# Macaron blocks on one core: router weights first, centered attention weights after the first routing, both norms of the late feed-forward ahead of its wide products

## The chip, the cores and the metric

One NeuronCore of a Trainium2 chip runs the whole program in one launch. The metric is the device time of one execution in microseconds (us), lower is better. A profiled execution also leaves a trace of every engine: TensorE (PE, with its weight loads as PEld), VectorE (DVE), ScalarE (ACT), GpSimd (POOL) and SyncE (SP), which issues most DMAs.

## The reference

The input is 4 x 1024 tokens with 128 channels, float32. Four layers follow one another; each is a half feed-forward, an attention, and the same half feed-forward again, all on a residual x. Each part first normalizes over the channels, without weights:

```python
def _layernorm(x, axis=-1, eps=1e-05):
    m = jnp.mean(x, axis=axis, keepdims=True)
    v = jnp.var(x, axis=axis, keepdims=True)
    return (x - m) / jnp.sqrt(v + eps)
...
    x = x + 0.5 * _L0_ffn_ref(_layernorm(x, axis=-1), ...)
    x = x + _L0_attn_ref(_layernorm(x, axis=-1), ...)
    x = x + 0.5 * _L0_ffn_ref(_layernorm(x, axis=-1), ...)
    x = x + 0.5 * _L1_ffn_ref(_layernorm(x, axis=-1), ...)
    x = x + _L1_attn_ref(_layernorm(x, axis=-1), ...)
    x = x + 0.5 * _L1_ffn_ref(_layernorm(x, axis=-1), ...)
```

Layer 0's feed-forward is a mixture of 8 experts of width 512: each token's normalized channels are multiplied by the router's weights, the two highest experts are taken, and their outputs are added with softmax weights. Layer 0's attention runs within a token, over its 16 heads of 8 channels. Layer 1's feed-forward is gated, `silu(gate) * up` of width 384 and a product down, with integer weights scaled by 1/127. Layer 1's attention is a softmax attention of 16 heads over 1024 tokens with rotated queries and keys. Layers 2 and 3 (another mixture, linear attentions, a recurrence) are not touched by the change.

## The kernel before

The residual lies in SBUF, channels on the partitions, as four tiles X[b] of 128 x 1024, one for each batch b. A norm is made on PE: a product with the centering matrix `c0["center"]` takes the mean away, ScalarE squares the result, products with a column of 1/128 give the variance, ScalarE takes the square root and VectorE the reciprocal; products with a broadcast of it (against the identity) spread it over the channels, and VectorE multiplies.

**Start of the program** (`run`). SP's queue gets the DMAs in the order in which they are written: the constants c0 (463.5 KB), the four x (512 KB each), then what the first two stages need: l0s (the router's weights, 128 x 8, 4 KB), l0a (layer 0's attention, 256 KB), l1f (layer 1's feed-forward, 576 KB) and more. l1f is read into a pool of its own, l1int, which is closed again when VectorE has scaled its three matrices (L601). Then the pool of the experts is opened. `moe["both"]` (L1387 to L1389) holds the centering matrix and, beside it, the centered router's weights, so that one product of X with it gives centered channels and logits at once.

**Layer 0** (`layer0`, `macaron`). A routing (`route`) takes one or two batches: products with "both", squares on ScalarE (L303), the square root (L305), scaled rows written to DRAM (L309), and then small VectorE steps that find each token's two experts and a list of blocks of 128 slots. An experts' task takes one block after another: SP loads the expert's weights (e_w, 578 KB), POOL gathers the rows (L454), PE and ScalarE compute, POOL scatters the result (L480). A combine reads both results of each token back and adds them to X. There are three groups of batches in each of the two mixtures: (0), (1), (2, 3) before the attention and (0, 1), (2), (3) after it. `centered` multiplies layer 0's attention weights with the centering matrix (`m["wqkvc"]`, read by `l0_attn` as the tasks "middle0" to "middle3").

The order in which these tasks' instructions are written comes from `lanes`: every task is a generator that yields its cost, each lane has a clock, and the lane with the lowest clock goes next. A task starts when the tasks it names are done, at a clock no lower than the lowest of the other active lanes. A scheduler then orders the instructions of every engine by what it expects to be ready, with the written order as priority, and places tiles when their buffers come free.

**Layer 1's attention** (`l1_attn`). PE's order is written by hand here (`manual_schedule`); the other engines' is not. Before the loop, `prepare(0)` makes batch 0's norm and projections, a generator with eleven yields; `spread` then lays queries and keys out with DMAs. The loop runs over units k: `greatest` finds the scores' row maxima (PE, and two VectorE reductions at L740 for each k), and eleven units later (LEAD) `scores` and `values` compute the exponentials and sums. "two" is a PSUM tile of two banks with two buffers; "s" has one bank and three buffers; "e" is an SBUF tile of 128 x 512 with ten buffers.

Layer 1's first feed-forward of the last batch (`self.late`) is not done in layer 0 but fed into this stage: `feed(b, hf)` is a generator for one half of the batch's columns. Its calls do, in order: centering, square and a copy (1); variance and reciprocal (2); broadcast and the normalized xn (3); a gate, a Silu, an up product and a multiplication for each of three hidden slices (4 to 6, the wide products); nothing (7); the product down and the addition to X (8). While `prepare(0)` runs, one call of a feed follows each of its yields from the third on; in the loop, one call of the feed at the head of the list follows each k, and one that is finished is removed.

Of the kernel before, what the change touches and what calls it, by code (L numbers as in the profile page):

```python
# [18 lines left out]
B, S, D = 4, 1024, 128  # L19
# [190 lines left out]
class Macaron:  # L210
# [446 lines left out]
    def l1_attn(self, m, c1, f):  # L657
# [6 lines left out]
        with ExitStack() as ctx:  # L664
# [150 lines left out]
            def feed(b, hf):  # L815
                c = slice(hf * HALF, (hf + 1) * HALF)
                bank, one = lambda: self.t(p2, [P, HALF], "s"), lambda: self.t(wp, [P, HALF], "e", bufs=10)
                cen, sq, xc = bank(), one(), one()
                self.mm(cen, self.c0["center"], self.X[b][:, c])
                nc.scalar.activation(sq, cen, AF.Square)  # L820
                v.tensor_copy(xc, cen)
                yield
                var = bank()[:, 0:4]
                for i in range(4):
                    self.mm(var[:, i : i + 1], sq[:, i * P : (i + 1) * P], self.c0["mean"][:, 0:1])
                std, r = self.t(self.lnp, [P, 4], "fstd"), self.t(self.lnp, [P, 4], "frstd")
                nc.scalar.activation(std, var, AF.Sqrt, bias=self.eps_ln)
                v.reciprocal(r, std)
                yield
                bc, xn, hs = bank(), one(), []  # L830
                for i in range(4):
                    self.mm(bc[:, i * P : (i + 1) * P], r[:, i : i + 1].to_broadcast([P, P]), self.c0["ident"])
                v.tensor_tensor(xn, xc, bc, ALU.mult)
                yield
                for i in range(HIDC):
                    g, u, s = bank(), bank(), one()
                    self.mm(g, f["wg"][:, i, :], xn)
                    nc.scalar.activation(s, g, AF.Silu)
                    self.mm(u, f["wu"][:, i, :], xn)
                    hs.append(one())  # L840
                    v.tensor_tensor(hs[i], s, u, ALU.mult)
                    yield
                yield
                o = bank()
                for i in range(HIDC):
                    self.mm(o, f["wd"][:, i, :], hs[i], start=i == 0, stop=i == HIDC - 1)
                self.add_half(b, c, o)

            late = [feed(b, hf) for b in self.late for hf in range(2)]
            for n, _ in enumerate(prepare(0)):  # L850
                if late and n >= 2:
                    next(late[0], None)
            for z in va:
                nc.gpsimd.memset(z, 0.0)
                nc.gpsimd.memset(z[:, :, :, 0:1], 1.0)
# [437 lines left out]
        self.lanes(blocks, back, *more(route))  # L1293

    def layer0(self, moe, m, right, enter, ffn):
        m["wqkvc"] = self.centered(m["wqkv"], 3 * D)
        early = right.enter_context(ExitStack())
        pa, pf = enter(early, "l0a"), enter(right, "l1f0", side="left")
        side, main = self.side, self.main
        self.late = [B - 1]  # L1300

        def swap():

            early.close()
            self.l1_rings(enter(self.rings, "l1rings", 1))
            yield 0

        def more(route):
            attn = lambda b, *after: (f"middle{b}", after, lambda: self.l0_attn(side, pa, m, b))
            last = lambda b, ps: (f"last{b}", (f"combine1{b}",), ffn(pf, ps, b))  # L1310
            return (
                [
                    route(0, (0,), ps=main), route(0, (1,)), route(0, (2, 3)),
                    *[attn(b, f"combine0{b}") for b in range(B)],
                    ("swap", (), swap), *[last(b, side) for b in range(B) if b not in self.late],
                ],
                [route(1, (0, 1), "middle0", "middle1", "combine03"), route(1, (2,), "middle2"), route(1, (3,), "middle3")],
            )


        groups = [(0,), (1,), (2, 3)], [(0, 1), (2,), (3,)]
        marks = {(0, (0,)): "_1", (0, (1,)): "_2", (0, (2, 3)): "_0", (1, (0, 1)): "_0", (1, (2,)): "_1", (1, (3,)): "_2"}
        self.macaron("l0", moe, AF.Gelu, groups, marks, more)
# [30 lines left out]
    def run(self, stages):  # L1354
        nc = self.nc
        self.X, self.ring, self.rings, self.late = [], {}, ExitStack(), []
        self.c0 = self.load("c0")
        for b in range(B):
            X = self.t(self.res, [P, S], f"x{b}")
            nc.sync.dma_start(out=X, in_=self.x[:, b * S : (b + 1) * S])  # L1360
            self.X.append(X)
        self.eps_ln = self.t(self.res, [P, 1], "eps_ln")
        nc.gpsimd.memset(self.eps_ln, LN_EPS)
        self.eps_gn = self.t(self.res, [P, 1], "eps_gn")
        nc.gpsimd.memset(self.eps_gn, GN_EPS)

        needs = {
            "l0": ("l0s", "l0a", "l1f"), "l1_attn": ("l1a", "c1"), "l2": ("l2s", "l2a", "c2"),
            "l3": ("l3f", "l3a", "c3"),
        }  # L1370
        tags = {"l1a": "attn_w", "l3a": "attn_w", "c1": "attn_c", "c2": "attn_c", "c3": "attn_c"}
        have = {}

        def weights(name):
            if name not in have:
                have[name] = self.l1_weights() if name == "l1f" else self.load(name, tag=tags.get(name))
            return have[name]

        sb = lambda name, bufs=2, **k: self.tc.tile_pool(name=name, bufs=bufs, reuse_waits="tile", **k)
        for n, name in enumerate(stages):  # L1380
            for s in stages[n : n + 2]:
                for w in needs[s]:
                    weights(w)
            if name in ("l0", "l2"):
                with self.psum("main", 4) as self.main, self.psum("side", 4) as self.side, sb(name + "moe") as self.fp:
                    moe = dict(weights(name + "s"))
                    moe["both"] = self.t(self.res, [P, P + NE], "both", bufs=2)  # L1387
                    nc.vector.tensor_copy(moe["both"][:, 0:P], self.c0["center"])
                    nc.scalar.copy(moe["both"][:, P:], self.centered(moe["rw"], NE))  # L1389
                    with ExitStack() as right:  # L1390
                        enter = lambda stack, name, bufs=2, side="right": stack.enter_context(sb(name, bufs, side=side))
                        m = dict(weights(name + "a"))
                        ffn = lambda wp, ps, b: lambda: self.l1_ffn(ps, wp, weights("l1f"), b)
                        if name == "l2":
                            self.c2 = weights("c2")
                        if name == "l0":
                            self.layer0(moe, m, right, enter, ffn)
                        else:
                            self.layer2(moe, m, right, enter, ffn)
            elif name == "l1_attn":  # L1400
                with sb("ln1") as self.lnp:
                    if not self.ring:
                        self.l1_rings(self.rings.enter_context(sb("l1rings", 1, side="right")))
                    self.l1_attn(weights("l1a"), weights("c1"), weights("l1f") if self.late else None)
                    self.rings.close()
            else:
                f, t, c3 = self.l3_ffn_weights(weights("l3f")), self.l3_time_weights(weights("l3a")), weights("c3")
                self.layer3(f, t, c3)
        self.rings.close()
        for b in range(B):  # L1410
            nc.sync.dma_start(out=self.out[:, b * S : (b + 1) * S], in_=self.X[b])
# [36 lines left out]
```

## Time and profile before

| | before |
|---|---|
| median of 3 runs | 3091.13 us (3089.98 to 3100.73) |
| the profiled execution, whole time | 3093.76 us |
| its span in the trace | 3092.0 us |
| mean granted TensorE clock | 0.915 |
| PE busy | 2709.1 us (88%) |
| VectorE, ScalarE, POOL busy | 59%, 53%, 25% |
| layer 0: from the first gather on POOL to the last scatter | 36.16 to 839.24 us |
| layer 1's attention: first scores to last exponential | 881.6 to 1935 us |

The page's slices, forty of equal length (77.3 us each), give the busy tenths of each engine, and the granted clock of TensorE in tenths of full speed:

```profile
PE   6868538778889999999999999998989996999997
PEld 5756416665643333333333333567878884334333
DVE  3586986864356776776677774362665632455763
ACT  4655425657715665565565666454444553344442
POOL 4666307553400000000000000047434562000110
PEclk8988768889989999999999999999989997798997
```

In each line a 9 stands for 90% or more. A line of the trace's timeline, as shown further on, gives the start in us, the length in us, the engine, the line of the code (L231 is the matmul helper `mm`), the operation, what it writes and reads with the tiles' names, its shapes and a count, and in brackets how long the engine had been idle before it and whose end released it.

### The profile page before, as it was taken

How to read it: one execution, taken by the hardware profiler on the slowest of the kernel's cores; microseconds unless marked ns; L12 is line 12 of the kernel's file. 1: busy time of each engine (PE TensorE's matmuls, PEld its weight loads, DVE VectorE, ACT ScalarE, POOL GpSimd, SP SyncE). 2: the span in 40 equal slices, each digit the busy share in tenths (PEclk: the TensorE clock that was granted, in tenths of full speed). 3: DMA queues.
4: the chain of work that ended last, by engine and by line, in shares of the span. 5: the costliest groups of instructions: out<-in, count | busy, mean ns of one | idle time of the engine just before them, and what ended most of it. 6: DMA issues, size and time to landing. Idle time of an engine off the chain costs nothing. (4 is left out here: it accounts for less than half of the span.)

```text
span 3092.0 us, 47511 instructions
## 1 busy us (share of the span) xinstructions
PE 2709.1 (88%) x17694; PEld 1564.1 (51%) x17694; DVE 1834.9 (59%) x3215; ACT 1623.9 (53%) x3633; POOL 780.5 (25%) x732
## 2 busy tenths in 40 slices
PE   6868538778889999999999999998989996999997
PEld 5756416665643333333333333567878884334333
DVE  3586986864356776776677774362665632455763
ACT  4655425657715665565565666454444553344442
POOL 4666307553400000000000000047434562000110
PEclk8988768889989999999999999999989997798997
DMA  7766316563500000000000000058665783000000
GB/s 247 220 182 189 113 52 199 165 201 108 156 14 5 5 7 4 5 6 5 19 5 6 1 1 1 20 179 267 203 191 170 229 283 103 1 1 0 7 7 14
DMA packets 122886, 277.57 MB, mean 90 GB/s; under 512 B 18016, under 2 KB 67296, under 8 KB 122528
## 3 DMA queue, kind: packets, MB, share of 16 engines
q1 hardware_dynamic: 101792, 231.77, 24.2%
q0 software_dynamic: 20864, 42.77, 4.9%
q8 instruction: 140, 2.29, 0.3%
q14 instruction: 90, 0.74, 0.1%
HBM read 238.43 MB, written 31.85 MB: 87 GB/s over the span
## 5 line engine op out<-in xcount | busy, mean ns | idle before, releaser
L740 DVE TENSOR_REDUCE nm<-two 128x2 f32<-128x1024 f32 x512 | 626.0, 1224 | 280.8 <-PE s L231 270.2
L763 ACT ACTIVATE e<-s 128x512 f32<-128x512 f32 x1024 | 555.8, 595 | 404.0 <-PE s L231 400.8
L468 ACT ACTIVATE e_h<-bank,e_w 128x128 f32<-128x128 f32 x1304 | 448.7, 367 | 397.2 <-PE bank L231 382.6
L231 PE MATMUL s<-qm,kz 32*128 32x512 f32 x2048 | 633.8, 642 | 0.8 <-ACT e L763 0.8
L231 PE MATMUL bank<-e_x,e_w 128*128 128x128 f32 x2608 | 535.5, 309 | 87.1 <-ACT e_h L468 54.7
L231 PE MATMUL two<-kz,qz 32*128 32x512 f32 x2048 | 578.0, 647 | 21.0 <-DVE nm L740 4.6
L454 POOL DMA_INDIRECT e_xg<-rows,g_source x326 | 330.6, 1014 | 753.7 <-DVE g_target L421 342.7
L231 PEld LDWEIGHTS bank<-e_x,e_w 128*128 128x128 f32 x2608 | 410.6, 203 | 166.9 <-ACT e_h L468 100.6
L231 PE MATMUL bank<-e_w,e_h 128*128 128x128 f32 x2608 | 463.3, 293 | 27.1 <-ACT e_h L468 17.2
L480 POOL DMA_INDIRECT res<-e_y,g_target x326 | 365.3, 1121 | 258.4 <-DVE e_y L479 106.4
L231 PEld LDWEIGHTS bank<-e_w,e_h 128*128 128x128 f32 x2608 | 379.3, 202 | 50.6 <-ACT e_h L468 30.7
L231 PE MATMUL o<-e,va 128*32 128x256 f32 x4096 | 328.3, 392 | 0.1
L231 PEld LDWEIGHTS o<-e,va 128*32 128x32 f32 x4096 | 81.0, 108 | 389.6 <-issue 369.6
L231 PEld LDWEIGHTS two<-kz,qz 32*128 32x128 f32 x2048 | 153.8, 184 | 228.9 <-issue 162.7
L231 PEld LDWEIGHTS s<-qm,kz 32*128 32x128 f32 x2048 | 206.9, 183 | 11.3 <-issue 7.7
L460 DVE COPY e_x<-bank 128x128 f32<-128x128 f32 x326 | 92.8, 285 | 192.0 <-PE bank L458 176.1
L479 DVE TENSOR_TENSOR e_y<-bank,e_w 128x128 f32<-128x128 f32 x326 | 93.9, 288 | 183.2 <-PE bank L231 163.3
L728 POOL COPY va<-vd 128x256 f32<-128x256 f32 x16 | 6.7, 431 | 624.6 <-PE o L231 537.9
L1177 POOL TENSOR_TENSOR z<-st,r 128x512 f32<-128x512 f32 x32 | 46.2, 1443 | 417.8 <-DVE st L1170 334.3
L458 PE MATMUL bank<-c,e_xg 128*128 128x128 f32 x326 | 96.5, 298 | 42.5 <-DMA e_xg<-rows,g_source 38.9
L468 ACT ACT_TABLE_LOAD x53 | 68.0, 1283 | 22.8 <-PE bank L231 16.6
L546 DVE TENSOR_TENSOR prod<-qkv 128x2048 f32<-128x2048 f32 x32 | 73.1, 2284 | 4.7 <-ACT qkv L538 4.7
(325 smaller groups left out, 3467.1 us busy)
## 6 DMA issues: line engine op xcount, KB each, us to landing
e_w<-in_l0m_dram SPq DMA_DIRECT2D x170, 578.0 KB
e_w<-in_l2m_dram SPq DMA_DIRECT2D x156, 578.0 KB
c_y<-res SPq DMA_DIRECT2D x32, 512.0 KB
rows<-g_xt SPq DMA_DIRECT2D x16, 512.0 KB
e_xg<-rows,g_source POOLq DMA_INDIRECT x326
res<-e_y,g_target POOLq DMA_INDIRECT x326
x<-in_x_dram SPq DMA_DIRECT2D x4, 512.0 KB
qz<-qd SPq DMA_DIRECT2D x64, 32.0 KB
```

What stands on the lines that cost most here:

```text
L231: self.nc.tensor.matmul(out, lhsT, rhs, start=start, stop=stop)
L454: nc.gpsimd.indirect_dma_start(out=xg, out_offset=None, in_=rows[:, :], in_offset=at(source[:, k : k + 1]))
L458: nc.tensor.transpose(tp, xg, self.c0["ident"])
L460: nc.vector.tensor_copy(x, tp)
L468: nc.scalar.activation(h[:, fc, :], o[:, fc, :], func, bias=w[:, 2 * FC * P + fc : 2 * FC * P + fc + 1])
L479: nc.vector.tensor_tensor(y, o, w[:, MOE_W - D :], ALU.add)
L480: ins = nc.gpsimd.indirect_dma_start(out=res[:, :], out_offset=at(target[:, k : k + 1]), in_=y, in_offset=None)
L546: v.tensor_tensor(pr, q.unsqueeze(2).to_broadcast(sh), k.unsqueeze(1).to_broadcast(sh), ALU.mult)
L728: nc.gpsimd.tensor_copy(va[n % RING][:, :, :, 1 : 1 + HD], dense[b, "vd"][:, :, 32 * g4 : 32 * g4 + 32].rearrange("p t (h d) -> p t h d", ...
L740: v.tensor_reduce(nm[:, it, h, 2 * pair : 2 * pair + 2], s, AX.X, ALU.max, negate=True)
L763: nc.scalar.activation(es[g], s, AF.Exp, scale=scale)
L1177: (pool if i else v).tensor_tensor(z, st[:, 0:HALF], r, ALU.mult)
```

## The change

Three edits. The router's weights are loaded ahead of the constants and of x. The centering of layer 0's attention weights is no longer the first thing in `layer0` but a task of the routing's lane, behind the first routing, at a cost of 0. And while `prepare(0)` runs, the calls at its yields 2 to 7 alternate between the two halves of the late feed-forward, so that calls 1 to 3 (the norm) of both are made before call 4 of the first; from yield 8 on the first half is called, as before.

```diff
@@ l1_attn
             for n, _ in enumerate(prepare(0)):
                 if late and n >= 2:
-                    next(late[0], None)
+                    next(late[n % 2 if n < 8 else 0], None)
@@ layer0
-        m["wqkvc"] = self.centered(m["wqkv"], 3 * D)
         early = right.enter_context(ExitStack())
...
         self.late = [B - 1]
+
+        def center():
+            m["wqkvc"] = self.centered(m["wqkv"], 3 * D)
+            yield 0
...
-                    route(0, (0,), ps=main), route(0, (1,)), route(0, (2, 3)),
+                    route(0, (0,), ps=main), ("center", (), center), route(0, (1,)), route(0, (2, 3)),
@@ run
         self.X, self.ring, self.rings, self.late = [], {}, ExitStack(), []
+        have = {"l0s": self.load("l0s")} if "l0" in stages else {}
         self.c0 = self.load("c0")
...
-        have = {}
```

## The prediction

> **What bounds the kernel now.** I read the page's engine shares and slices first: PE is busy 88% of 3092.0 us, and from slice 12 to 25 it stands at 9 tenths or more. But the change touches two short places, and PE's share there is another. So I read the timeline of the start (0 to 36 us) and of the hand-over from layer 0 to layer 1's attention (845 to 927 us), then the windows for the granted clock.
>
> The start, timeline of VectorE and of ScalarE (start, length, what, and in brackets the idle time and its releaser):
>
> ```profile
> 4.25 0.36 DVE L1388 COPY both<-c 128x128 f32<-128x128 f32 x2 [4.25 <-DMA c<-in_c_dram]
> 13.00 0.36 DVE L601 TENSOR_SCALAR l1f_wg<-l1f 128x384 f32<-128x384 int32 x1 [8.39 <-DMA l1f<-in_l1f_dram]
> 13.28 0.35 DVE L601 TENSOR_SCALAR l1f_wu<-l1f 128x384 f32<-128x384 int32 x1
> 13.55 0.35 DVE L601 TENSOR_SCALAR l1f_wd<-l1f 128x384 f32<-128x384 int32 x1
> ```
> ```profile
> 11.73 0.17 ACT L263 COPY cw<-bank 128x8 f32<-128x8 f32 x1 [9.70 <-PE bank L231]
> 11.93 0.20 ACT L1389 COPY both<-cw 128x8 f32<-128x8 f32 x1
> 13.27 0.48 ACT L263 COPY cw<-bank 128x384 f32<-128x384 f32 x1 [1.15 <-PE bank L231]
> 13.99 0.28 ACT L303 ACTIVATE g_xt<-bank 128x128 f32<-128x128 f32 x1 [0.24 <-DVE l1f_wd L601]
> ```
>
> The router's weights land at 11.1 us (PE's first matmul, at 11.13, waits for that DMA alone), behind four 512 KB loads of x. Yet the first square of the routing, at 13.99, was not released by PE. Its releaser is VectorE's scaling of l1f_wd, which ended at 13.90. The square reads nothing of l1f: g_xt lies in memory that the raw l1f held (the pool l1int is closed before the routing's pool opens), so it must wait for the last read of it. And that read waits for the l1f DMA, which landed at 13.0.
>
> The hand-over, timeline of PE alone, consecutive lines:
>
> ```profile
> 852.73 2.06 PE L231 MATMUL s<-x,c 128*128 128x512 f32 x2
> 855.52 1.87 PE L231 MATMUL s<-c,e 128*128 128x1 f32 x8 [0.73 <-ACT e L820]
> 857.25 3.76 PE L231 MATMUL two<-c,rstd 128*128 128x128 f32 x16
> 860.80 1.12 PE L231 MATMUL s<-c,frstd 128*128 128x128 f32 x8
> ```
> ```profile
> 887.93 2.08 PE L231 MATMUL s<-x,c 128*128 128x512 f32 x2
> 889.93 1.96 PE L231 MATMUL two<-kz,qz 32*128 32x512 f32 x8
> 891.83 1.05 PE L231 MATMUL s<-c,e 128*128 128x1 f32 x8
> 893.22 2.55 PE L231 MATMUL two<-kz,qz 32*128 32x512 f32 x8 [0.34 <-DVE nm L740]
> 895.70 2.08 PE L231 MATMUL s<-c,frstd 128*128 128x128 f32 x8
> ```
>
> PE's order is written by hand here, so a step on PE holds up all behind it. The first block is the norm of the late feed-forward's first half (s) woven with attention's own norm (two). The second is the norm of its second half, inside the score loop: before k = 11 no exponentials run, and each k needs two VectorE reductions of 1.224 us (L740), so 2.45 us a step is the floor.
>
> Windows, the granted clock in the third column from the end (PE busy is the first figure after the window's length):
>
> ```profile
> 885.00:887.00 2.00, 2.00 (x8) 0.50 (x4) 1.39 (x2) 0.00 (x0) 0.00 (x0) 0.50 0.33 49
> 905.00:908.00 3.00, 3.00 (x12) 1.02 (x11) 2.96 (x5) 0.52 (x1) 0.00 (x0) 1.00 0.00 0
> ```
>
> PE is full in both, at half clock in the first and full clock in the second.
>
> **Part 1, the router's weights first.** Moved: one DMA of 4 KB on SP's queue. It is issued at 3.28 now; then it comes before c (0.75) and the four x (1.20 to 3.23). Its issue took 0.67 us, c's 0.39, so everything behind it is issued 0.4 to 0.7 us later. Removed: PE's wait to 11.13, about 5 us of it, since c has landed by 4.25 and x follows. What is late next is the square's wait. The bytes ahead of l1f stay the same (463.5 + 4 x 512 + 4 + 256 KB), so l1f lands at 13.0 plus about 0.45, and the first square starts near 14.4. The 5 us are thus not gained. What is: the eleven squares before the square root's table load take from 13.99 to 17.65, at a pitch of 0.253 us where PE is ahead (14.88 is followed by 15.54 because it is not). With PE far ahead they take 11 x 0.253 = 2.8 instead of 3.66, a gain of 0.85. Net: -0.4 us at the routing, and so at the first gather (36.16), behind which the experts run in a chain. Ends: -2 (the table load also moves in front of the three squares that aren't the first batch's) to +1.
>
> **Part 2, attention's weights centered later.** Two matmuls (1.65 us), one copy on ScalarE (0.48), no DMA. Now they lie in front of the first square, in time that waits for l1f anyway: removing them gains nothing. Afterwards they are a task of the routing's lane behind route00. The trace has no such placement. Their first reader is middle0, beyond 200 us. If both fall inside the routing's chain they cost at most 2.1 us, if in idle PE and ScalarE time (PE was busy 4.7 of the 20 us after 20) nothing; I take 0. By the lanes' yields the extra task shifts its lane's clock from 25 to 26, so eleven expert blocks instead of ten are written ahead of route01's first part; a few parts later two neighbours swap, and from there the order written is that of before. One block is one POOL gather and scatter, 0.97 + 0.99 + two gaps of 0.3 = 2.57 us. experts00 has 23 of them (59 us), and experts01 needs route01 only after them, so the cover is ample.
>
> **Part 3, both halves' norms in front.** Before, the calls between prepare's yields 2 to 9 were the first half alone, whole. Now they alternate: centering of half 0 and 1, variance of 0 and 1, broadcast of 0 and 1, then half 0's three wide steps. PE's new order: attention's variance, centering 0, centering 1, attention's broadcast, variance 0, variance 1, t1, broadcast 0, t2, broadcast 1, t1 of k, wide 0, t2 of k, wide 1, v, wide 2.
>
> Prologue. Attention's broadcast sits behind one more centering (2.06), but no longer behind variance 0, which cost 0.73 of waiting and 1.87. It could start at 854.8 + 2.06 = 856.9 instead of 857.25. The added centering waits for nothing: VectorE wrote x's second half at 849.70. Queued behind the broadcast: xn, the first rotated product (864.80 now, behind broadcast 0 and wide 0; then behind two variances only), POOL's sum for k at 876.61, the spreading DMAs, the first scores at 881.61. At half clock throughout (broadcast 3.76, variances 1.87 each) the product starts near 864.4, and following the order down with these durations kd comes 1.3 us earlier. At full clock from about 857 (16 transposing matmuls of this size took 1.95 at 877.68) it is 2.4. The two centerings back to back make the second likelier: **-2.0**.
>
> Here the Trainium skill, "TensorE: Matmul & The Clock Gate", section on the HAM clock gate, says that about 3.4 us of sustained work brings the full clock. The row at 885 speaks against counting on it: PE busy 2.00 of 2.00 at 0.50, with matmuls of 32 rows. By the rule every step of the loop from k = 1 on would be at full clock; by the row only those behind full-height matmuls. I take the row.
>
> Loop. From one k's first reduction to the next, the trace gives 3.19, 5.46, 2.45, 5.44, 4.04, 2.98, 3.58, 2.48, 5.61, 2.4, 6.1 for k = 0 to 10, 43.75 in all. Removed: what centering and broadcast add over the floor, 3.01 at k = 1 and 2.99 at k = 3; the variance at k = 2 added nothing. Added: half 0's last product and its add (L253, 0.69), at k = 1. Its six matmuls took 2.74 at full clock (914.67), so 5.5 at half; I take 4.2, the clock rising meanwhile, with 2.0 for the scores: 6.2 for the step. The wide steps at k = 2, 3, 4 then take 3.4, 3.3, 3.3 (2.15 of PE plus 1.14 of scores), the second half's last product at k = 6 4.4, and k = 8, which keeps the shift's transposes, 3.8. Sum: 3.19 + 6.2 + 3.4 + 3.3 + 3.3 + 2.45 + 4.4 + 2.45 + 3.8 + 2.4 + 6.1 = 41.0, **-2.75**. Ends: -4.5 (k = 1 all at full clock) and +1.4 (half clock through k = 2: 7.5 and 6.2).
>
> Two table loads go: half 1's square root and its Silu, each 1.283 us, at 890.65 and 893.20. "ScalarE: Activation LUTs", table sets, says to batch by set and prices a switch at 2.66 us, so 5.3 for two. In the trace ScalarE sat idle 9.36 us before the square ahead of the first, and 7.36 between the second's norm and the Silu: **0** beyond what the loop's steps already hold. Buffers: both norms hold six of the ten e tiles and at most the three s banks, so nothing new waits for them. From k = 11 on PE sets the pace, and the shift goes to the end.
>
> **Sum.** -0.4 - 2.0 - 2.75 = -5.15. The profiled run's span 3092.0 becomes 3086.9 (its whole time was 3093.76); from the median 3091.13 it gives **3086.0**.
>
> **Rivals.**
> (a) The norm is only moved (20%): the clock stays at half through k = 1 and 2, and the loop's +1.4 eats the prologue: 3091.13 - 0.4 - 1.3 + 1.4 = 3090.8. For it: half clock in the row above; against: the centering at 887.93 was followed by full clock at 891.5.
> (b) Slower (19%): the order of layer 0. All engines but PE in l1_attn are ordered by a scheduler that saw other start times and one more task. If each of the six expert groups starts one POOL step of 2.57 later, 15.4 is added: 3101.4. It decides from two such steps on (5.15 / 2.57). For it: POOL waited 77 us in all for e_y and 114 us once for g_source in layer 0, so its chain has no slack at the hand-overs; against: the written order differs in two places only.
> (c) The same the other way (13%): the first routing 2 us earlier, and four steps of 2.57 saved at hand-overs: 3086.0 - 1.6 - 10.3 = 3074.1.
>
> The forecast keeps 48%, its own range 3082 to 3091. The range is 3074 to 3101: both order cases up to the times given. A difference of 0.5% (15.5 us) is about what can be told from no change. Faster by more needs (c) with six steps instead of four: 8%. Slower by more needs eight steps in (b), about half of its chance: 10%. Within: 82%.
>
> **What would show it.** In the changed profile: the first square still released by l1f_wd and not before 13.9 (if it starts at 8 us, part 1 is wrong, and gains 5); the first gather within 2 us of 36.16; one centering pair on PE behind the other, the k sum earlier by 1 to 3 us against the last combine; no square root between the first scores and k = 10; k = 0 to 10 in 39 to 43 us. The prediction is wrong if layer 0's end moves by over 5 us.

## The result, and the profile after

In 13 runs of each on one chip the changed kernel took 3089.25 us (3082.03 to 3093.46) and the kernel before 3097.48 (3087.35 to 3100.75). The ratio is 0.9979, with an interval of 0.997 to 0.9988: 6.5 us less, at least 3.7 and at most 9.3. The forecast was 5.15 us less, 3086.0 us from a median of 3091.13 in three runs; ten more runs moved that median to 3097.48. The profiled execution of the changed kernel took 3093.46 us with a span of 3091.7, so this pair of traces differs by only 0.3 us in all. The traces are therefore read stage by stage, not by their ends.

The page's slices for PE and the granted clock hardly change:

```profile
PE   6868538778899999999999999998989986999997
...
PEclk8988768889989999999999999999999998798997
```

**The start.** Timeline of VectorE and of ScalarE, changed kernel:

```profile
5.22 0.36 DVE L1391 COPY both<-c 128x128 f32<-128x128 f32 x2 [5.22 <-DMA c<-in_c_dram]
13.14 0.36 DVE L601 TENSOR_SCALAR l1f_wg<-l1f 128x384 f32<-128x384 int32 x1 [7.55 <-DMA l1f<-in_l1f_dram]
13.42 0.35 DVE L601 TENSOR_SCALAR l1f_wu<-l1f 128x384 f32<-128x384 int32 x1
13.69 0.35 DVE L601 TENSOR_SCALAR l1f_wd<-l1f 128x384 f32<-128x384 int32 x1
```
```profile
13.40 0.48 ACT L263 COPY cw<-bank 128x384 f32<-128x384 f32 x1 [7.07 <-PE bank L231]
14.07 0.28 ACT L303 ACTIVATE g_xt<-bank 128x128 f32<-128x128 f32 x1 [0.19 <-DVE l1f_wd L601]
```

The first square comes at 14.07 (13.99 before), with the same releaser. The constants land 0.97 us later, l1f 0.14 later. PE's timeline shows what became of the early router weights:

```profile
5.34 0.57 PE L231 MATMUL bank<-l0s,c 128*128 128x8 f32 x2 [5.34 <-DMA c<-in_c_dram]
6.88 1.70 PE L231 MATMUL bank<-both,x 128*128 128x136 f32 x6 [0.98 <-DMA x<-in_x_dram]
11.72 1.65 PE L231 MATMUL bank<-l0a,c 128*128 128x384 f32 x2 [3.14 <-DMA l0a<-in_l0a_dram]
13.16 4.67 PE L231 MATMUL bank<-both,x 128*128 128x136 f32 x20
```

PE starts 5.8 us earlier, makes three of the router's products (six passes; the trace has two for each product), and then stands. The centering of the attention's weights (bank<-l0a,c) is not behind the routing at all: written later, it was still put early in PE's order, and it waits there for its own DMA. The first gather is at 36.79, against 36.16.

**The hand-over.** PE's timeline of the changed kernel, consecutive lines:

```profile
854.13 3.47 PE L231 MATMUL s<-x,c 128*128 128x512 f32 x4
857.44 1.95 PE L231 MATMUL two<-c,rstd 128*128 128x128 f32 x16
859.22 1.84 PE L231 MATMUL s<-c,e 128*128 128x1 f32 x16
860.93 1.96 PE L231 MATMUL two<-xn,attn_w 128*128 128x512 f32 x4
```

Both centerings stand together (four passes), both variances behind attention's broadcast, and that broadcast takes 1.95 us instead of 3.76. The windows around it, the first of before and the second of after (PE busy first after the length, granted clock third from the end), show half clock and nearly full clock:

```profile
857.20:860.80 3.60, 3.60 (x17) 3.60 (x18) 0.18 (x1) 1.55 (x2) 0.00 (x0) 0.50 0.00 0
857.00:860.00 3.00, 3.00 (x26) 2.73 (x24) 1.86 (x3) 0.60 (x1) 0.00 (x0) 0.97 0.00 0
```

Attention's first projection starts 3.5 us behind the broadcast's start, where it had been 7.55 (857.25 to 864.80). POOL's sum for k, from which the keys of the first scores are laid out, follows. One projection of before, then the sum of before and that of after:

```profile
864.80 1.88 PE L231 MATMUL two<-xn,attn_w 128*128 128x512 f32 x4
876.61 2.35 POOL L713 TENSOR_TENSOR kd<-rot,rot 128x1024 f32<-128x1024 f32 x1 [2.80 <-DVE rot L711]
872.89 2.35 POOL L713 TENSOR_TENSOR kd<-rot,rot 128x1024 f32<-128x1024 f32 x1 [3.70 <-DVE rot L711]
```

Then the start of the loop in the changed kernel:

```profile
877.88 6.40 PE L231 MATMUL two<-kz,qz 32*128 32x512 f32 x16 [1.11 <-POOL va L728]
884.21 4.66 PE L231 MATMUL s<-e,l1f_wd 128*128 128x512 f32 x6
888.80 1.14 PE L231 MATMUL two<-kz,qz 32*128 32x512 f32 x8
```

Windows of the changed kernel:

```profile
882.00:885.00 3.00, 3.00 (x7) 1.00 (x6) 2.05 (x3) 0.00 (x0) 0.00 (x0) 0.50 0.31 46
885.00:887.00 2.00, 2.00 (x4) 0.74 (x3) 0.55 (x1) 0.00 (x0) 0.00 (x0) 0.50 0.33 49
```

The first half's product down, moved to k = 1, takes 4.66 us, most of it at half clock, where two reductions of VectorE need 2.45.

Layer 0 ended at different times in the two executions, so the hand-over is best counted from attention's variance product (849.45 and 850.86), which both have at the same place of PE's order. The loop is the time from the first scores to unit k = 11, where the first product with the shifted queries (s<-qm,kz) starts.

| us | first gather | from the variance: POOL's sum for k | first scores | k = 11 | loop |
|---|---|---|---|---|---|
| before | 36.16 | 27.16 | 32.16 | 76.43 | 44.27 |
| after | 36.79 | 22.03 | 27.02 | 71.37 | 44.35 |

So the stretch ahead of the loop gives 5.1 us, the loop nothing. At k = 11 the changed kernel stands 3.65 us earlier in absolute time, since its layer 0 had ended later: the variance came 1.41 us later.

### The profile page after: what moved, and what is told of

Read it like the earlier page. It is cut to its first block, busy times and chain, and to the rows that moved or that the text cites. A ratio compares the mean times of both kernels' runs of the same rounds, so it can differ in the third digit from the quotient of the medians.

```text
span 3091.7 us, 47508 instructions
## 1 busy us (share of the span) xinstructions
PE 2715.0 (88%) x17694; PEld 1567.9 (51%) x17694; DVE 1834.0 (59%) x3215; ACT 1622.7 (52%) x3631; POOL 782.0 (25%) x732
```

## The experiments

They ran in three groups, each on another chip. The kernel before took 3227.44, 3228.63 and 3211.76 us there, with a wider spread, and layer 0 ends near 886 to 901 us, not 838. So times are compared within a group only. The table has each trace's places, all in us as in the table above, and the mean granted clock within the loop; the first four rows are one group, the next four the second, the last four the third. For before and after of the first chip that clock is 0.81 in both.

| label | first square | first gather | sum for k | first scores | k = 11 | loop | clock | ratio to before (interval) |
|---|---|---|---|---|---|---|---|---|
| e1_feed_only | 15.26 | 38.07 | 22.67 | 27.66 | 72.19 | 44.53 | 0.81 | 0.9993 (0.998 to 1.0006) |
| e2_head_only | 13.96 | 35.70 | 27.16 | 32.16 | 76.14 | 43.98 | 0.81 | 0.9998 (0.9987 to 1.001) |
| e3_center_pinned | 13.85 | 35.82 | 22.80 | 27.80 | 75.59 | 47.79 | 0.76 | 0.9989 (0.9974 to 1.0003) |
| e4_l1f_own | 8.71 | 30.94 | 23.36 | 28.36 | 74.54 | 46.18 | 0.78 | 0.9966 (0.9947 to 0.9984) |
| c2_before | 13.77 | 36.11 | 26.93 | 31.93 | 76.02 | 44.09 | 0.81 | |
| e6_down_ahead | 13.76 | 36.05 | 22.67 | 29.05 | 69.36 | 40.31 | 0.83 | 0.9979 (0.9967 to 0.999) |
| c2_after | 13.77 | 35.68 | 22.57 | 27.57 | 72.08 | 44.51 | 0.81 | 0.9998 (0.9977 to 1.0019) |
| e8_l1f_own_down | 7.80 | 30.72 | 22.94 | 29.33 | 72.76 | 43.43 | 0.77 | 0.9945 (0.9925 to 0.9965) |
| r1_feed_only | 13.56 | 35.95 | 22.87 | 27.87 | 75.68 | 47.81 | 0.76 | 0.9996 (0.9983 to 1.0008) |
| r2_head_only | 14.13 | 36.39 | 27.73 | 32.73 | 78.48 | 45.75 | 0.74 | 0.9995 (0.9979 to 1.001) |
| r3_after | 14.55 | 36.39 | 22.93 | 27.92 | 75.73 | 47.81 | 0.76 | 0.9992 (0.9976 to 1.0008) |
| r4_l1f_own_down | 7.65 | 29.89 | 22.80 | 29.19 | 67.96 | 38.77 | 0.89 | 0.9925 (0.9906 to 0.9944) |

**The two parts apart.** My theory: the hand-over makes the gain, the head none. The rival: the head or a new order of layer 0 makes it. Part 3 alone is the one-line edit of `l1_attn` on the kernel before; the head alone is the changed kernel without that line.

```diff
-                    next(late[0], None)
+                    next(late[n % 2 if n < 8 else 0], None)
```

> The kernel before with the alternating feed calls alone; router's load and centering as before. If the gain is made at the hand-over: layer 0 as before (first gather at 36.2, last scatter at 838.3, within 1 us), the first scores 5 us earlier against the last scatter (38.3 us behind it instead of 43.3), k = 0 to 10 about 44 us as before, the time 3 to 7 us below the kernel before. If the gain came from the head or from a new order of layer 0: 0 to -2 us.

> The changed kernel with the feed calls as before: only the router's load first and the centering behind the first routing. If the head gives nothing, since the squares still wait for l1f's scaling and the constants land later: first gather at 36.8, last scatter near 839.9, the time 0 to +2 us against the kernel before. If the head or layer 0's order carries the gain: -4 us or more.

The places separate cleanly: the sum for k stands at 22.67 with part 3 alone, and at 27.16 with the head alone, as in the kernel before on the first chip. The whole times do not: both intervals hold 1. On this chip 3 to 5 us (0.1 to 0.15%) is about the half-width of an interval, so no total here proves either part, and neither excludes a gain of 3 to 4 us. The run of e1 also shows how far the start itself varies: with the old order of loads its square came at 15.26, since l1f landed 1.3 us later than in the trace of before, and its gather at 38.07.

**The centering's place.** It stalls PE from 8.6 to 11.7 us in the changed kernel. Does that pace the squares?

```diff
-            m["wqkvc"] = self.centered(m["wqkv"], 3 * D)
+            m["wqkvc"] = self.centered(m["wqkv"], 3 * D, self.routed)
...
+            self.tc.add_manual_dep(i, after.name, order, reason="behind the first routing")
```

(`self.routed` is the last product of the first routing, `i` the centering product.)

> The changed kernel, the centering of the attention's weights ordered on PE behind the first routing's last product. In the changed kernel PE's order has that centering after six products of the router, and it waits there for its weights until 11.7. If this is what paces the squares: the squares follow one another at 0.25 us from 14.1, the square root's table load comes at 16 to 17 instead of 18.26, the first gather at 34.5 to 35.8. If the centering's place does not matter: 36.8. In both cases the squares still wait for l1f.

A miss: the squares are not faster, the square root comes at 19.05 (19.56 in the changed kernel, 18.47 in e2), the gather at 35.82. PE's timeline of this run:

```profile
5.11 0.56 PE L231 MATMUL bank<-l0s,c 128*128 128x8 f32 x2 [5.11 <-DMA c<-in_c_dram]
6.93 1.70 PE L231 MATMUL bank<-both,x 128*128 128x136 f32 x6 [1.26 <-DMA x<-in_x_dram]
14.27 3.01 PE L231 MATMUL bank<-both,x 128*128 128x136 f32 x10 [5.64 <-ACT g_xt L306]
```

With nothing in its way PE again makes three products and then waits, now for ScalarE's squares. In `route` the eight products of a batch share three PSUM tiles. The wait fits an order that takes one product of each tile first, after which the second one of a tile waits until ScalarE has read the first; the trace does not number the tiles, so this is a reading. Of one batch, PE is three products ahead here, not eight. And ScalarE waits for l1f. The gather, at 35.82, is as late as that of e2 (35.70), so the centering's place costs nothing: its stall lies under that wait.

**The wait for l1f.** The raw matrices go into the buffer that later holds attention's constants, instead of a pool whose memory the routing inherits.

```diff
-        with self.tc.tile_pool(name="l1int", bufs=1) as ip:
-            raw = self.load("l1f", ip)
+        raw = self.load("l1f", tag="attn_c")
```

> The changed kernel with the raw l1f read into the space of the later attention constants, not into a pool whose memory the routing takes over. If the shared memory is what holds the squares: the first square near 8 us instead of 14.07, not released by VectorE's scaling, and the first gather 2 to 6 us earlier, 31 to 35. If the squares wait for something else that ends at the same time: first square at 14, gather at 36.8. The whole time follows by as much only if layer 0 passes it on.

As expected. ScalarE's timeline of this run:

```profile
5.55 0.20 ACT L1391 COPY both<-cw 128x8 f32<-128x8 f32 x1
8.71 0.28 ACT L303 ACTIVATE g_xt<-bank 128x128 f32<-128x128 f32 x1 [2.97 <-PE bank L231]
```

The first square now waits for PE, which waits for x. It comes 5.3 us before that of e2 in the same group, the gather 4.8 us before. This is the head's gain that the change itself left covered. The whole time is 0.9966 of the kernel before, 11 us less (5 to 17). That fits a gain at the gather that is passed on, with some of the hand-over's beside it; it does not tell the two apart.

**The loop's loss.** A second trace of before and of after in one group, and the changed kernel with the first half's product down ahead of the first scores:

```diff
             for n, _ in enumerate(prepare(0)):
                 if late and n >= 2:
                     next(late[n % 2 if n < 8 else 0], None)
+            for _ in range(2):
+                next(late[0], None)
```

> The kernel before once more, for a second trace of it on the same chip as the runs beside it. From attention's variance product on PE: POOL's sum for k 27.2 us later, first scores 32.2, unit k = 11 76.4, if these stages repeat.

> The changed kernel once more: first scores 27 to 28 us behind the variance product, k = 11 71 to 76, against 32.2 and 76.4 in the kernel before on this chip; time 3 to 9 us below it. If the gain at the hand-over is lost in the loop: k = 11 as in the kernel before.

> The changed kernel, with the first half's product down and its addition put behind the last projection, ahead of the first scores, instead of behind k = 1. If that product at half clock (4.66 us and more at k = 1, where two reductions need 2.45) is what keeps the loop from gaining: first scores 1.5 to 3 us later (29 to 30 us behind the variance product), k = 0 to 10 in 38 to 40.5 us instead of 44, k = 11 2 to 4 us earlier than in the changed kernel (67.5 to 69.5 behind the variance). If the loop is held by something else: k = 11 at 71 to 75, as there, or later by what the first scores lose.

The places of before and after repeat those of the first chip within 0.7 us (76.02 and 72.08); the whole time of c2_after does not show them, its interval holds 1. The edit of e6 does what was expected of it: first scores 1.5 us later than in c2_after, loop 40.31, k = 11 2.7 us earlier. PE's timeline and windows of e6_down_ahead:

```profile
939.06 2.74 PE L231 MATMUL s<-e,l1f_wd 128*128 128x512 f32 x6
941.72 1.62 PE L231 MATMUL two<-kz,qz 32*128 32x512 f32 x8
944.20 2.26 PE L231 MATMUL two<-kz,qz 32*128 32x512 f32 x8 [0.86 <-DVE nm L740]
```
```profile
939.00:941.00 2.00, 2.00 (x6) 0.95 (x5) 0.69 (x1) 0.05 (x1) 1.13 (x4) 1.00 0.29 43
941.00:943.00 2.00, 2.00 (x10) 0.60 (x8) 0.76 (x2) 0.00 (x0) 0.00 (x0) 1.00 0.34 49
943.00:945.00 2.00, 1.14 (x5) 0.30 (x4) 2.00 (x2) 0.00 (x0) 0.00 (x0) 1.00 0.33 49
968.00:971.00 3.00, 3.00 (x9) 1.18 (x8) 2.19 (x4) 0.00 (x0) 0.00 (x0) 0.52 0.00 0
```

The product fills time in which PE was idle: in every trace without this edit the first scores start 5.0 us behind POOL's sum for k, which is the sum itself (2.35) and the DMAs that lay it out (SP issues them from 875.26 to 877.89 in the changed kernel), and PE idles 1.1 to 2.0 us ahead of them. The product costs 2.74 us instead of 4.66 to 5.49, and the clock does not fall at the loop's start, only 26 us further on.

**Both together, and once more.**

> The changed kernel with both: the raw l1f in the later constants' space, and the first half's product down ahead of the first scores. If the two gains are independent: first gather 5 us earlier (31), k = 11 67.5 to 69.5 behind the variance product, the time 8 to 14 us below the kernel before. If layer 0 absorbs the earlier start: only the 2 to 4 us of the loop below the changed kernel.

> The feed calls alone, again, since 22 runs left it open whether they gain at all (0.998 to 1.0006). If the hand-over makes the whole gain: k = 11 4 to 5 us earlier behind the variance product, and a ratio of 0.998 to 0.999. If the head makes it: 1.000.

> The head alone, again. If it gives nothing: ratio 0.9995 to 1.001 and the first gather within 0.7 us of 36.1. If it carries a part of the gain: 0.998 to 0.999.

> The changed kernel beside its two parts. If the parts add up: the product of their ratios, near 0.998 to 0.9985; if they hinder each other: 0.9995 or more.

> The changed kernel with the raw l1f in its own place and the product down ahead of the first scores, beside the changed kernel. If both gains hold: ratio 0.994 to 0.997, below the changed kernel; if they were this chip's noise: the changed kernel's ratio.

The version with both edits is the fastest: 0.9945 and 0.9925 of the kernel before, intervals clear of 1 and, in both groups, of the changed kernel's own. Its gather comes 5.4 us earlier than in c2_before (30.72 against 36.11). At k = 11 the two traces disagree. r4 stands where it was expected (67.96, against 75.73 in r3). e8 does not: at 72.76 it is 3.3 us ahead of c2_before, and 0.7 behind the changed kernel in its own group. The clock fell again before its second product down, at k = 5:

```profile
949.71 5.08 PE L231 MATMUL s<-e,l1f_wd 128*128 128x512 f32 x6
```

So the two gains add up in one of two traces. The whole times fell by more than was expected of e8 (17.6 us, 8 to 14 expected) and of r4 (25.4 us), and by more than these places account for. A part goes with the clock: the runs of e8 and r4 have a mean granted clock of 0.9066 and 0.9107, those of the kernel before beside them 0.9034 and 0.9073. A line through the runs of the kernel before alone has about 2 us of time for 0.001 of clock; by that estimate some 6.5 us of each difference go with the clock. Whether the edits raised it is not shown. The rest lies in layer 0's body and the later layers, and single traces cannot place it: from the first gather to the last scatter, one kernel took 861.41 us in e1 and 853.73 in r1. Its cause stays open.

The repeats of the parts left their totals open again: r1, at 0.9996, misses the 0.998 to 0.999 expected of it, r3, at 0.9992, lies between its two cases, and all three intervals hold 1. On these chips the change's own gain cannot be told from nothing, nor from the 0.9979 of the first chip, while the places repeat.

## Why the prediction was right, and where it was not

The interval of the measured gain, 3.7 to 9.3 us, holds the forecast 5.15, and 3089.25 us lies between 3082 and 3091. Of the five signs that the prediction named for the profile three came: the square is still released by l1f_wd, the gather lies within 2 us of 36.16, and no square root stands in the loop. Two did not: the sum for k is 5.1 us earlier, not 1 to 3, and the loop is outside 39 to 43 us. So the total is right in part by luck.

**The start of the routing: mechanism right.** The square stays released by l1f_wd, and the 5 us of the early router weights are not gained. e4 shows that the wait for the shared memory is the cover: with a buffer of its own for l1f the squares start 5.3 us earlier. Inside it one reason was wrong: that PE would be "far ahead" and the eleven squares would take 2.8 us. They took 4.19 (14.07 to the table load at 18.26). e3 shows that PE can be three products of a batch ahead, and the squares' pace follows the products': in e2 and c2_after a pass falls from 434 to 279 ns between 14.4 and 14.8 us and the square root comes at 18.47 and 18.42; in the first trace of after the passes take mostly 434 ns and it comes at 19.56, with the same order. The forecast -0.4 at the gather measured +0.63 in the first pair, -0.43 in the second group and +0.44 in the third (r2 and r3 against r1, which has the old head): its sign is not settled.

**The centering: cost 0, by luck of the cover.** It was written behind the routing, and in PE's order it moved by six passes only. The prediction placed it inside the routing's chain or in idle time behind it; it stayed in the idle time ahead of the first square.

**The prologue: right in kind, mis-sized.** -2.0 was taken, 2.4 the most; measured at POOL's sum for k: -5.1 in the first pair of traces (before and after), -4.4 in the second group, -4.5 and -4.9 for part 3 alone beside the head alone in the same group. In the first pair, attention's broadcast started 1.2 us earlier, not 0.35: the passes of the two centerings follow one another every 0.86 us at half clock, and the last one ran partly at full clock (3.47 us for the four, not 2 x 2.06). The broadcast then took 1.8 us less. And the first projection came 2.25 us closer behind it: broadcast 0 and wide 0 no longer lie between, and the two variances that do took 1.84 us together, where the walk at half clock had 1.87 for each. Of these 5.3 us POOL's sum for k kept 5.1, since from the projection to the sum both traces need nearly the same (11.81 us before, 11.96 after). How the walk at full clock came to 2.4 is not on record, so which of its later steps took the rest stays open.

**The loop: wrong.** -2.75 was forecast, with ends of -4.5 and +1.4; measured +0.1 in the first pair, +0.4 in the second group, and beside the head alone of the same group +0.6 (e1), +2.1 (r1 and r3), +2.2 (e4) and +3.8 (e3). The steps from one k's first reduction to the next:

| k | 0 | 1 | 2 | 3 | 4 | 5 | 6 | 7 | 8 | 9 | 10 | sum |
|---|---|---|---|---|---|---|---|---|---|---|---|---|
| forecast | 3.19 | 6.2 | 3.4 | 3.3 | 3.3 | 2.45 | 4.4 | 2.45 | 3.8 | 2.4 | 6.1 | 41.0 |
| after | 3.22 | 7.19 | 2.98 | 3.57 | 2.98 | 2.46 | 4.96 | 2.48 | 4.53 | 3.40 | 6.04 | 43.8 |
| r3_after | 2.50 | 8.38 | 2.98 | 3.57 | 2.99 | 2.46 | 8.31 | 2.48 | 4.05 | 3.41 | 6.50 | 47.6 |

The wide steps at k = 2 to 4 are near the forecast (9.5 us against 10.0). In the first pair these steps are 2.8 us longer than forecast: 1.0 at k = 1, where the product down was sized at 4.2 us and took 4.66 (up to 5.49 in other traces), and 2.3 at k = 6 to 9. Of these, 0.6 at k = 6 came at full clock, so there the step was sized too short; 0.7 at k = 8 and 1.0 at k = 9 lie where the clock fell to half, which the prediction did not have. The scores of k = 9 and 10 in the changed kernel, with a window of their clock, and the same two in the kernel before:

```profile
911.82 2.67 PE L231 MATMUL two<-kz,qz 32*128 32x512 f32 x8 [0.47 <-DVE nm L740]
915.22 3.21 PE L231 MATMUL two<-kz,qz 32*128 32x512 f32 x8 [0.73 <-DVE nm L740]
```
```profile
915.00:918.00 3.00, 2.78 (x8) 1.00 (x8) 1.95 (x3) 0.00 (x0) 0.00 (x0) 0.50 0.00 0
```
```profile
917.34 1.14 PE L231 MATMUL two<-kz,qz 32*128 32x512 f32 x8
919.80 2.26 PE L231 MATMUL two<-kz,qz 32*128 32x512 f32 x8 [1.31 <-DVE nm L740]
```

At k = 6 a second fall makes the difference between traces. The second product down took 2.84 us where the clock was full (after, e1), and 5.24 us in e3, at half clock:

```profile
960.11 5.24 PE L231 MATMUL s<-e,l1f_wd 128*128 128x512 f32 x6
```

So what failed in this term is the clock: it was to rise during k = 1 and not to fall again. With the changed order of calls, the loop is as long as its mean clock is low: 44.35 to 44.53 us at 0.81, 46.18 at 0.78, 47.79 to 47.81 at 0.76. Why the clock falls once more ahead of k = 6 in some traces and not in others is not shown. e6, e8 and r4 take the product out of k = 1; their loops are 40.31, 43.43 and 38.77 us, each below the changed kernel's in its group (44.51 and 47.81).

**The sum.** Prologue and loop were forecast at -4.75 together and measured -5.06 in the first pair, -3.94 in the second group, -2.75 in the third (r3 beside r2) and -0.55 in e3 beside e2. Two errors of opposite sign met, and that the first two sums lie near the forecast is luck. Two rules of the Trainium skill that the prediction names were rightly not counted. By the one on table sets ("ScalarE: Activation LUTs", "Table sets") the two loads would be worth 5.3 us; both are gone (none stands between 861.38 and 924.27), and the loop is no shorter. By the one on sustained work ("TensorE: Matmul & The Clock Gate", "The HAM clock gate") every step from k = 1 on would be at full clock, as the prediction works out; in the changed kernel PE counted as busy 2.00 of 2.00 us at 0.50. Of the rivals, (a), where the loop eats the prologue, describes the traces with a loop near 47.8: there 2.1 of 4.8 us (r3 beside r2) and 3.8 of 4.4 (e3 beside e2) are eaten. (b) and (c), six later or four earlier hand-overs of layer 0, are not seen in the first pair: from the first gather to the last scatter it is 802.1 us before and 803.1 after.

## What to carry to other kernels

Before a load is moved forward, look at what else its reader waits for: a pool that inherits another's memory can hold the reader longer than the data do. Writing a step later does not make a scheduler place it later, so look at the engine's own order. Work put into an idle stretch ahead of a loop can gain twice, once for the stretch and once where PE's clock then stays up in the loop, as in e6 and r4. Work put into a loop of short steps is paid at that loop's clock, not at the clock of the row it was priced from.

## What the runs showed of the hardware

The granted clock fell to half within the first units of the loop although PE counted as busy (0.77 in 880 to 882, 0.50 in 882 to 887 in the changed kernel). Its work there was products of 32 rows, of which the first sixteen took 6.40 us; later, eight take 1.14. The six full-height passes of k = 1 had almost ended before the clock rose again.

The kernel before makes a product down of the same six passes ahead of its first scores, too, but then idles:

```profile
875.10 2.74 PE L231 MATMUL s<-e,l1f_wd 128*128 128x512 f32 x6
877.68 1.95 PE L231 MATMUL two<-attn_w,xn 128*128 128x128 f32 x16
881.61 6.39 PE L231 MATMUL two<-kz,qz 32*128 32x512 f32 x16 [1.98 <-POOL va L728]
```

In all eleven traces with 1.1 to 2.0 us of idle time just ahead of the first scores, the clock fell 1.7 to 4.6 us behind their start. In the three traces with the product in that place and no idle time (e6, e8, r4) it stayed at 1.00 for 16 to 30 us behind their start, in e6 even through a window where PE was busy 1.14 of 2.00 us. That the missing idle time is the reason is argued, not shown: in these three the scores also start later behind the sum for k, 6.4 us instead of 5.0, and may wait less for their data.

In the first 11 us of a program the clock column reads 1.00 in every trace, but the traces hold no record of the clock there. The first record comes at 11.0 us (r4) to 40.0 (e3); it is at 14.4 in before, 14.7 in e2 and 17.5 in after. Up to it a pass of the router's product takes mostly 434 ns; behind it, in these three, mostly 279. There the length of a pass tells more than the column does.
